# Loading later tiles of x one at a time, in halves from a second queue, with three regular output slots, in a pairwise bilinear kernel

## The chip, the cores and the metric

The kernel runs on one core of a Trainium2 chip. The metric is the device time of one execution in microseconds (us), taken without the profiler; the profile is of a separate execution and its span is measured from the first to the last instruction.

## What is computed

The input x has 4096 rows of 32 fields with 64 numbers each, W is 64 x 64, all float32. Every field is multiplied by W, and then every field i is multiplied, number by number, with the transformed field j for each of the 496 pairs i < j:

```python
vid = jnp.einsum('bfd,de->bfe', x, W)
idx_i, idx_j = jnp.triu_indices(F_, k=1)
return x[:, idx_i, :] * vid[:, idx_j, :]
```

The input is 33.6 MB and the output 520.1 MB, so writing the output is most of what the kernel moves.

## The kernel before

**Tiles.** The host lays x out so that the 128 partitions hold two batch halves of 64 embedding numbers, and so that a tile t (16 of them) holds 128 batch rows of each half. One field of one tile is a unit of 128 float32 per partition (512 B per partition, 64 KB in all). A tile of x is 32 units, its output 496 units (pairs).

**Memory.** One large SBUF tile, `mem` (L130), of 445 units holds both the tiles of x and the finished products waiting to be written. Where each tile of x lies is given by XPLACE (L25). Where each group of products (a slot) lies is given by the table SLOTS (L28), 80 pairs of (size in pairs, first unit): sizes run from 43 to 127 pairs, and places were fitted around the tiles of x that are in memory at the time. A slot's place is used again by later slots, and by tiles of x.

**Work on a tile** (loop at L155). TensorE multiplies the 32 fields by W, in 16 matmuls (two partition halves times eight banks, L162), into `vid`, one PSUM tile of 32 units, all of PSUM. VectorE multiplies (L186): `products` (L69) cuts the pairs of a tile into rectangular pieces, first all pairs among fields 0 to 15 (120 pairs), then fields 0 to 15 against 16 to 31 (256 pairs), then the pairs among fields 16 to 31 (120 pairs). A piece that would run over the end of a slot is cut there, so the slot table decides how many instructions there are (407). When the last pair of a slot is written, SyncE (SP) issues the slot's store (L189), one transfer with one row of up to 65,024 B per partition.

**Loads.** Every load also stands on SP's queue. The tiles of x come in the three groups of GROUPS (L20): the first group at the start (tile 0 in two halves with w between them, then tiles 1-2, 3-4 and 5, L138 to L153), the second (tiles 6-7 and 8-10) behind the products of tile 4, the third (tiles 12-11 and 15-13) behind those of tile 9 (L192 to L194). A load moves up to three tiles at once.

**Order.** SP's instructions keep the order in which the program writes them (`manual_schedule`, L122), so loads and stores form a single queue. Semaphore waits follow from overlaps: a product waits for the stores that still read its place, a load waits for the products and stores that use its place, a matmul waits for the products that still read its bank of `vid` and for its tile of x.

Of the kernel before, what the change touches and what calls it, by code (L numbers as in the profile page):

```python
# [16 lines left out]
UNITS = 445  # L17


GROUPS = [  # L20
    [[0], [1, 2], [3, 4], [5]],
    [[6, 7], [8, 9, 10]],
    [[12, 11], [15, 14, 13]],
]
XPLACE = [285, 317, 349, 381, 413, 0, 285, 317, 349, 381, 413, 128, 96, 64, 32, 0]  # L25


SLOTS = [  # L28
    (127, 32), (126, 159), (63, 32), (64, 95), (84, 159), (63, 32),
    (74, 243), (84, 159), (95, 32), (71, 243), (116, 127), (95, 32),  # L30
    (106, 243), (116, 127), (95, 32), (106, 243), (116, 127), (95, 32),
    (127, 243), (116, 127), (95, 32), (127, 243), (116, 127), (43, 370),
    (95, 32), (95, 127), (63, 222), (95, 32), (84, 127), (74, 211),
    (84, 32), (95, 116), (74, 211), (116, 0), (95, 116), (74, 211),
    (116, 0), (95, 116), (105, 211), (105, 0), (105, 105), (105, 211),
    (105, 0), (105, 105), (127, 211), (105, 0), (105, 105), (127, 211),
    (105, 0), (106, 105), (56, 211), (95, 267), (51, 362), (107, 160),
    (73, 267), (73, 340), (84, 160), (84, 244), (95, 340), (84, 160),
    (95, 244), (105, 340), (84, 160), (96, 244), (105, 340), (105, 128),
    (106, 233), (105, 339), (127, 96), (116, 223), (106, 339), (127, 96),  # L40
    (116, 223), (106, 339), (127, 64), (127, 191), (127, 318), (127, 32),
    (127, 159), (120, 286),
]


PAD = 24
# [2 lines left out]

STARTS = [0, *accumulate(n for n, _ in SLOTS)]  # L50


def by_block():


    def within(lo):
        yield "step", lo, 2, 1, 0
        for k in range(2):
            yield "step", lo, 4, 2, k
        for i in (lo, lo + 8):  # L60
            yield "row", i + 4, i, 4, 4
        yield "row", lo + 8, lo, 8, 8

    yield from within(0)
    yield "row", 16, 0, 16, 16
    yield from within(16)


def products(blocks, at=0):  # L69

    for kind, a, b, c, d in blocks:
        if kind == "row":
            rows, n, i0, di, j0, dj = c, d, b, 0, a, 1
        else:
            rows, n, i0, di, j0, dj = 16 // b, c, a, b, a + c + d, b
        r = k = 0
        while r < rows:
            room = STARTS[bisect_right(STARTS, at)] - at
            if k or room < n:
                m, w = 1, min(n - k, room)  # L80
            else:
                m, w = min(rows - r, room // n), n
            yield at, m, w, i0 + r * di + k, di, j0 + r * dj, dj
            at += m * w
            if k + w == n:
                r, k = r + m, 0
            else:
                k += w
# [10 lines left out]
@with_exitstack  # L99
def pairwise_bilinear_kernel(  # L100
    ctx: ExitStack,
    tc: tile.TileContext,
    x0: bass.AP,
    x: bass.AP,
    w: bass.AP,
    out: bass.AP,
):

    nc = tc.nc
    NT = sum(len(tiles) for group in GROUPS for tiles in group)
    F = x0.shape[1] - PAD0
    D = P // 2
    NP = F * (F - 1) // 2

    BANK = 512 // C


    ctx.enter_context(tc.manual_schedule(engines={mybir.EngineType.SP}))  # L122

    const = ctx.enter_context(tc.tile_pool(name="const", bufs=1))
    psum = ctx.enter_context(
        tc.tile_pool(name="ps", bufs=1, space=bass.MemoryType.PSUM)
    )
    vid = psum.tile([P, F, C], F32)

    mem = const.tile([P, UNITS, C], F32)  # L130


    w2 = const.tile([P, D], F32)


    for lo in (0, F // 2):
        place = XPLACE[0] + lo
        nc.sync.dma_start(out=mem[:, place : place + F // 2, :], in_=x0[:, lo : lo + F // 2, :])  # L138
        if lo == 0:
            nc.sync.dma_start(out=w2, in_=w)  # L140
    loaded = 1

    def load(tiles):
        nonlocal loaded
        n = len(tiles) * F
        place = XPLACE[tiles[0]]
        at = (loaded - 1) * F
        nc.sync.dma_start(out=mem[:, place : place + n, :], in_=x[:, at : at + n, :])
        loaded += len(tiles)

    groups = iter(GROUPS)
    for tiles in next(groups)[1:]:
        load(tiles)  # L153

    for t in range(NT):  # L155
        xt = mem[:, XPLACE[t] : XPLACE[t] + F, :]


        for b in range(0, F, BANK):
            for h in range(2):  # L160
                half = slice(h * D, (h + 1) * D)
                nc.tensor.matmul(  # L162
                    vid[half, b : b + BANK, :],
                    lhsT=w2[half, :],
                    rhs=xt[half, b : b + BANK, :],
                    start=True,
                    stop=True,
                )

        for at, m, w, i, di, j, dj in products(by_block(), t * NP):  # L170
            slot = bisect_right(STARTS, at) - 1
            n = m * w
            begin, end = STARTS[slot], STARTS[slot + 1]
            ot = mem[:, SLOTS[slot][1] : SLOTS[slot][1] + SLOTS[slot][0], :]
            o = ot[:, at - begin : at - begin + n, :]
            if m == 1:
                left = xt[:, i : i + w, :]
                right = vid[:, j : j + 1, :].to_broadcast([P, w, C])
            else:
                o = o.rearrange("p (m w) c -> p m w c", m=m)  # L180
                right = vid[:, j : j + (m - 1) * dj + 1 : dj, :].unsqueeze(2).to_broadcast([P, m, w, C])
                if di == 0:
                    left = xt[:, i : i + w, :].unsqueeze(1).to_broadcast([P, m, w, C])
                else:
                    left = xt.rearrange("p (m d) c -> p m d c", d=di)[:, i // di : i // di + m, i % di : i % di + w, :]
            nc.vector.tensor_tensor(o, left, right, ALU.mult)  # L186
            at += n
            if at == end:
                nc.sync.dma_start(out=out[:, begin:end, :], in_=ot)  # L189


        if t + 2 == loaded < NT:  # L192
            for tiles in next(groups):
                load(tiles)  # L194


_INS = ["r_x", "L0_rec_W"]
# [42 lines left out]
```

## Time and profile before

| | |
|---|---|
| time, median of 3 runs | 1288.43 us (1288.34 to 1288.59) |
| span of the profiled execution | 1287.0 us |
| VectorE busy | 1087.8 us (85%), 407 instructions |
| TensorE busy | 225.4 us (18%), 512 matmuls |
| DMA queue of SP | 553.69 MB, 12,960 packets, 99.7% of 16 engines' span |
| read from and written to HBM | 33.59 MB and 520.09 MB |

The page gives busy time of each compute engine, the busy share in 40 equal slices of the span, the bytes and time of each DMA queue, the chain of waits that ended last, and the costliest groups of instructions with what ended the idle time before them. A second view, of stages, gives for a stretch of the span the busy time of each engine, the clock granted to TensorE, the mean busy share of the 16 DMA engines and the GB/s they moved. The trace also holds a record of each single DMA packet: its queue, start, duration and bytes; a packet here is one partition's row of a transfer. Each transfer over 128 partitions is 8 packets on each of the 16 DMA engines and ends with one 4 B packet on each.

### The profile page before, as it was taken

How to read it: one execution, taken by the hardware profiler on the slowest of the kernel's cores; microseconds unless marked ns; L12 is line 12 of the kernel's file. 1: busy time of each engine (PE TensorE's matmuls, PEld its weight loads, DVE VectorE, ACT ScalarE, POOL GpSimd, SP SyncE). 2: the span in 40 equal slices, each digit the busy share in tenths (PEclk: the TensorE clock that was granted, in tenths of full speed). 3: DMA queues.
4: the chain of work that ended last, by engine and by line, in shares of the span. 5: the costliest groups of instructions: out<-in, count | busy, mean ns of one | idle time of the engine just before them, and what ended most of it. 6: DMA issues, size and time to landing. Idle time of an engine off the chain costs nothing.

```text
span 1287.0 us, 1744 instructions
## 1 busy us (share of the span) xinstructions
PE 225.4 (18%) x512; PEld 41.6 (3%) x512; DVE 1087.8 (85%) x407; POOL 0.2 (0%) x4
## 2 busy tenths in 40 slices
PE   4031221312013013030313111103131121302000
PEld 1000000000000000000000000000000000000000
DVE  6799999998948399899999887369999998989960
POOL 0000000000000000000000000000000000000000
PEclk8555555556555555565655555555555555655555
DMA  9999999999999999999999999999999999999998
GB/s 411 432 427 431 442 432 430 437 434 433 435 422 419 425 430 433 438 432 438 428 439 436 428 440 421 427 430 435 434 438 428 439 435 439 434 430 437 430 434 368
DMA packets 12969, 553.79 MB, mean 430 GB/s; under 512 B 1568, under 2 KB 1568, under 8 KB 1568
## 3 DMA queue, kind: packets, MB, share of 16 engines
q1 hardware_dynamic: 12960, 553.69, 99.7%
q8 instruction: 4, 0.07, 0.0%
q14 instruction: 5, 0.04, 0.0%
HBM read 33.59 MB, written 520.09 MB: 430 GB/s over the span
## 4 chain that ended last, share of the span: by engine, by line
DMA 49%; DVE 44%; issue 3%; PE 0%; another core or an unknown queue 0%; DVEq 0%; SPq 0%
DMA out_dram<-mem 49%; DVE mem L186 44%; PE vid L162 0%; DMA w<-in_L_rec_W_dram 0%; DVEq L228 0%; DVEq L186 0%; SPq L138 0%
## 5 line engine op out<-in xcount | busy, mean ns | idle before, releaser
L186 DVE TENSOR_TENSOR mem<-mem,vid 128x1024 f32<-128x1024 f32 (+16 forms) x407 | 1087.8, 2748 | 155.0 <-DMA out_dram<-mem 143.3
L162 PE MATMUL vid<-mem,w 64*64 64x512 f32 x512 | 225.4, 1004 | 949.5 <-DVE mem L186 883.2
L162 PEld LDWEIGHTS vid<-mem,w 64*64 64x64 f32 x512 | 41.6, 198 | 1131.6 <-DVE mem L186 1033.3
L208 POOL MEMSET const-bfloat16-1.0<- 128x1 bf16 x1 | 0.1, 101 | 0.0
L208 POOL MEMSET const-uint8-127<- 128x1 uint8 x1 | 0.1, 101 | 0.0
L208 POOL MEMSET const-float32-0.0<- 128x1 f32 x1 | 0.1, 98 | 0.2 <-issue 0.2
L208 POOL MEMSET const-float32-1.0<- 128x1 f32 x1 | 0.1, 98 | 0.0
## 6 DMA issues: line engine op xcount, KB each, us to landing
out_dram<-mem SPq DMA_DIRECT2D x12, 8128.0 KB, 35.1
out_dram<-mem SPq DMA_DIRECT2D x13, 6720.0 KB, 32.9
out_dram<-mem SPq DMA_DIRECT2D x14, 6080.0 KB, 31.0
out_dram<-mem SPq DMA_DIRECT2D x9, 7424.0 KB, 31.6
out_dram<-mem SPq DMA_DIRECT2D x8, 5376.0 KB, 23.7
out_dram<-mem SPq DMA_DIRECT2D x6, 6784.0 KB, 34.6
out_dram<-mem SPq DMA_DIRECT2D x4, 4736.0 KB, 26.2
mem<-in_r_x_dram SPq DMA_DIRECT2D x4, 4096.0 KB, 21.8
```

The lines of the kernel that those rows point to most:

```text
L162: nc.tensor.matmul(vid[half, b : b + BANK, :], lhsT=w2[half, :], rhs=xt[half, b : b + BANK, :], start=True, stop=True,)
L186: nc.vector.tensor_tensor(o, left, right, ALU.mult)
L208: nc = _bacc.Bacc("TRN2", target_bir_lowering=False, num_devices=1, dynamic_dma_scratch_size=1024)
```

## The change

Only the first five tiles are loaded at the start, all on SP as before. Each of the other eleven is loaded on its own, in two halves of 16 fields (1 MB, rows of 8 KB per partition), and these 22 loads are issued from ScalarE's queue, which otherwise has nothing to do. A half is issued as soon as the half that lay in its place has been used for the last time: fields 0 to 15 after 376 pairs of a tile (the first two blocks), fields 16 to 31 at the end of it. From tile 5 on there are two places for x, used in turn, so tile t+2 goes where tile t was; tiles 5 and 6 take the places of tiles 0 and 1.

The slots become regular: three of equal size, used in turn. While the first tiles still hold memory they have 95, then 105 and 116 pairs, from tile 5 on 127, which with two places for x fill the 445 units. The host no longer permutes the tiles. What is computed, and the order of pairs in a tile, stay the same.

```diff
-GROUPS = [
-    [[0], [1, 2], [3, 4], [5]],
-    [[6, 7], [8, 9, 10]],
-    [[12, 11], [15, 14, 13]],
-]
-XPLACE = [285, 317, 349, 381, 413, 0, 285, 317, 349, 381, 413, 128, 96, 64, 32, 0]
-SLOTS = [
-    (127, 32), (126, 159), (63, 32), (64, 95), (84, 159), (63, 32),
...
-]
+HEAD = [[0], [1], [2, 3, 4]]
+FIRST_HALF = 376
+
+def place_of(t):
+    return (381, 413, 285, 317, 349)[t] if t < 5 else (381, 413)[(t - 5) % 2]
+
+def slots():
+    n = 0
+    left = 16 * 496
+    out = []
+    while left:
+        done = n // 496
+        room = (95, 95, 95, 105, 116)[done] if done < 5 else 127
+        k = len(out) % 3
+        size = min(room, left)
+        out.append((size, k * room))
+        n += size
+        left -= size
+    return out
+
+SLOTS = slots()
...
-    ctx.enter_context(tc.manual_schedule(engines={mybir.EngineType.SP}))
+    ctx.enter_context(tc.manual_schedule(engines={mybir.EngineType.SP, mybir.EngineType.Activation}))
...
-    def load(tiles):
-        nonlocal loaded
-        n = len(tiles) * F
-        place = XPLACE[tiles[0]]
-        at = (loaded - 1) * F
-        nc.sync.dma_start(out=mem[:, place : place + n, :], in_=x[:, at : at + n, :])
-        loaded += len(tiles)
-
-    groups = iter(GROUPS)
-    for tiles in next(groups)[1:]:
-        load(tiles)
+    def load(queue, tile, lo, n):
+        place = place_of(tile) + lo
+        at = (tile - 1) * F + lo
+        queue.dma_start(out=mem[:, place : place + n, :], in_=x[:, at : at + n, :])
+
+    for tiles in HEAD[1:]:
+        load(nc.sync, tiles[0], 0, len(tiles) * F)
+
+    later = {}
+    for t in range(5, NT):
+        before = t - 5 if t < 7 else t - 2
+        later.setdefault(before, t)
...
             nc.vector.tensor_tensor(o, left, right, ALU.mult)
             at += n
+            if at == t * NP + FIRST_HALF and t in later:
+                load(nc.scalar, later[t], 0, F // 2)
             if at == end:
                 nc.sync.dma_start(out=out[:, begin:end, :], in_=ot)
...
-        if t + 2 == loaded < NT:
-            for tiles in next(groups):
-                load(tiles)
+        if t in later:
+            load(nc.scalar, later[t], F // 2, F // 2)
...
-    x = x[:, [t for group in GROUPS for tiles in group for t in tiles]]
```

## The prediction

> **What bounds the kernel now.** I read the page first, slices before shares. Its second part shows the 16 DMA engines full in all slices, VectorE (DVE) with holes:
>
> ```profile
> DVE  6799999998948399899999887369999998989960
> ...
> DMA  9999999999999999999999999999999999999998
> GB/s 411 432 427 431 442 432 430 437 434 433 435 422 419 425 430 433 438 432 438 428 439 436 428 440 421 427 430 435 434 438 428 439 435 439 434 430 437 430 434 368
> DMA packets 12969, 553.79 MB, mean 430 GB/s; under 512 B 1568, under 2 KB 1568, under 8 KB 1568
> ```
>
> The rate is flat near 433 GB/s but for four places: the first slice, the 12th to 14th, the 25th and 26th, and the last (a slice is 32 us). The third and fourth parts say whose bytes these are and that the end hangs on them:
>
> ```profile
> q1 hardware_dynamic: 12960, 553.69, 99.7%
> ...
> HBM read 33.59 MB, written 520.09 MB: 430 GB/s over the span
> ...
> DMA 49%; DVE 44%; issue 3%; PE 0%; another core or an unknown queue 0%; DVEq 0%; SPq 0%
> ```
>
> The chain's 44% of DVE is no second bound: it hops over DVE because a store cannot be issued before its products exist, while older stores keep the engines busy. Of DVE's idle time before L186 (155.0 us) 143.3 us wait for a store to free a slot. So each microsecond of DMA time added or removed arrives at the end one for one, and only that.
>
> The trace's single packets give the price. A 65,024 B store packet takes 2,400 ns, one of 32,256 B 1,194 ns: 0.03677 ns per byte plus 8 ns per packet; the 4 B packet that signals a transfer's end takes 9 ns. Per engine: 553.69 MB / 16 x 0.03677 = 1272.4 us, 90 transfers x 8 packets x 8 ns = 5.8 us, 90 x 9 ns = 0.8 us: 1279.0 us. The first packet starts at 2.6 us, the last ends 0.6 us before the span's end. The packets' excess over this price, summed and divided by 16, is 4.7 us. Together 1286.9 us, against a span of 1287.0 (1288.4 as timed).
>
> **Where the excess sits** answers what a read among writes costs. It is 0.9 us in the opening loads; nearly all the rest lies in the two later visits to the loads: 1.97 us from 380 to 440 us, 1.18 us from 800 to 840 us. In each, the last store packets before the loads and the last load packets before the stores take about 0.9 us too long on every engine (at the second visit's entry less). The stages show it too (columns: stage, its length, busy times, PE clock, DMA share, GB/s):
>
> ```profile
> 30.00:380.00 350.00, 65.60 (x142) 10.52 (x138) 314.67 (x125) 0.00 (x0) 0.53 1.00 433
> 380.00:426.00 46.00, 10.09 (x24) 2.65 (x24) 33.01 (x15) 0.00 (x0) 0.54 1.02 421
> 426.00:800.00 374.00, 64.90 (x144) 11.10 (x144) 332.52 (x125) 0.00 (x0) 0.53 1.00 433
> 800.00:833.00 33.00, 6.13 (x16) 1.77 (x16) 13.09 (x3) 0.00 (x0) 0.55 1.02 424
> ```
>
> 421 for 433 GB/s over 46 us is 1.3 us lost, 424 over 33 us 0.7 us. "Busy" stays at 1.00: a turn from writing to reading counts as busy time, so only GB/s and packet durations reveal it.
>
> The trace also holds nine reads that another queue slipped between stores:
>
> ```profile
> q8 instruction: 4, 0.07, 0.0%
> q14 instruction: 5, 0.04, 0.0%
> ```
>
> (five of 8 KB, four of 16 KB, once the program runs). At 143.4 us an 8 KB fetch keeps one engine for 0.31 us, its transfer alone, but the engine's next store takes 2,151 instead of 1,796 ns, 0.36 us more. Three of the other 8 KB fetches cost 0.35 or 0.36 us in the same way, one 0.27. A 16 KB fetch lasts 0.88 to 0.96 us instead of 0.61, and the next store loses 0.38 to 0.41 us more: some 0.7 us. At 164.1 us the fetch stands between two packets of one and the same store (59,392 B on both sides, and only one such transfer near): a second queue gets in after a packet, not after a transfer.
>
> **What the Trainium skill says.** "DMA: Bandwidth & Descriptors", section "Where 436 GB/s comes from", puts the ceiling of the fabric at 435.2 GB/s; the trace agrees (433 to 434 in stages of stores alone; 0.03677 ns per byte is 435). Its section "Issuing engines are not separate DMA queues" says that transfers from several issuing engines share the same 16 DMA engines and interleave: ScalarE's queue brings no bandwidth. Its section "Queues, rings and completion order" says that an engine goes round-robin over queues with work, at packet granularity, and that a packet is typically 9 to 17 descriptors. The fetch at 164.1 us shows a switch inside a transfer, so I take single records of the trace as the unit; whether the 8 records of an 8 KB-row load stay together, no trace here shows.
>
> **The change part by part.**
>
> 1. Slots: 80 stores become 68; SLOTS gives 16 of 95 pairs, 5 of 105, 4 of 116, 42 of 127, one of 93. Same bytes. Loads go from 9 and one for w to 26 and one: 95 transfers instead of 90, so 5 x (8 x 8 + 9) ns = 0.4 us more.
> 2. DVE: 379 products instead of 407 (counted from both slot tables). From the 128- and 1,024-element rows (283 and 1,214 ns) the fixed part is 0.15 us: 28 x 0.15 = 4 us less. Hidden: DVE has 155 us of idle time.
> 3. Starving the DMA: DVE fills 127 pairs in 17.4 us (first stretch, 11.5 to 29.0 us); their store takes 8 x 2.40 = 19.2 us. While DVE refills one of three slots, two stores (38.4 us) are queued, so 17.4 us plus some 2 us of launch (0.7 us issue to 2.6 us first packet) fits. Where slots grow, a new one overlaps the second old one only with its last 11 to 22 pairs, some 3 us of DVE beside at least 14 us of queued store. Cost 0.
> 4. Start: 5 tiles queued instead of 6. Before, 12.6 MB of loads end near 33.9 us; 2.1 MB less ends near 29. The first slot of 95 pairs is full at 11.5 + 95 x 0.138 = 24.6 us and its store can begin near 26.5. Cost 0, with 2 us to spare. Tile 5's bytes only move.
> 5. The added wait: a load on ScalarE waits for the last DVE product (and matmul) that reads its half tile. Behind it on ScalarE stand only later loads; stores stay on SP. The half is needed one tile later, at least 70 us, and lands after 8 x (2.40 + 0.31 + 0.36) = 25 us even if it alternates with stores. No one waits. Cost 0.
> 6. The two visits go: 3.2 us less.
> 7. The price: 22 loads of 1 MB, each 8 packets of 8 KB per engine, in a second queue while the store queue is never empty. If each packet gets in singly, 22 x 8 = 176 reads per engine are inserted among stores. At 0.36 us each: 63 us; at the 0.7 us of the 16 KB fetches: 123 us; if reads already queued are prefetched behind a 2.4 us store, perhaps 0. I take 0.36: same packet size, and a second queue as here.
>
> Sum: 1288.4 + 0.4 - 3.2 + 63 = 1348.6; I say 1348.
>
> **The rivals.**
> - Loads stay together: each engine drains the 8 packets of a load before it goes back. Then 22 visits at the 1.58 us mean of the two measured: 35 us, 1288.4 + 35 - 3 = 1320. With 0.36 us a visit 1293, with 1.97 us 1329. For it: the skill's packet of several descriptors. Against: the fetch inside a store.
> - Costly singles: 0.7 us each, 1288 + 123 - 3 = 1408. For it: all 16 engines now turn at once, as in the visits. Against: no 8 KB fetch cost more than 0.36.
> - Hidden turns: with two queues one engine reads ahead while it writes; no cost per load, and the visits' 3.2 us are saved: 1288.4 + 0.4 - 3.2 = 1285.6, just faster than before; with the opening's excess gone too 1284.7. No more can be won, for 1279 us is bytes. For it: the fetch's own record shows no latency. Against: the store after it does. If half the saving is lost, the time stays within 0.2%.
>
> **How the numbers follow.** Singles at 0.36 to 0.5 us (1345 to 1375): 0.45. Costly singles (to 1413): 0.13. Loads together (1293 to 1329): 0.29. Little or no cost, within 0.2%: 0.07. Faster: 0.05. Anything above 1413: 0.01. The range, 1306 to 1413, leaves out the last three and the cheap end of "together", some 0.07. Slower 0.88, same 0.07, faster 0.05.
>
> **What would show it.** DVE's busy time near 1084 us, its waits still for stores, no wait of PE for loads: steps 2 to 5. The DMA share still 9 in every slice, but GB/s near 405 in the tiles that load (0, 1 and 5 to 13) and 433 in tiles 2 to 4, 14 and 15, mean near 411: step 7. Packets: 8 KB loads near 0.31 us, the store after each 0.36 us too long, load and store alternating on an engine. Eight loads in a row mean the first rival; 433 GB/s throughout means hidden turns. Slices with DMA below 9 mean starving, and step 3 or 4 is wrong.

## The result and the profile after

The changed kernel takes 1295.7 us (1295.4 to 1297.2), the kernel before, run beside it, 1288.5 us. The ratio is 1.0057, with a 95% interval of 1.0043 to 1.0071: slower by 7.2 us, where 60 us were forecast.

From the page of the changed kernel, the lines that answer to those shown of before (the last line is from the view of its DMA issues):

```profile
DVE  6998889599799999788787888888888878789860
...
DMA  9999999999999999999999999999999999999997
GB/s 406 435 427 438 427 431 433 433 421 429 437 437 430 440 405 457 406 457 419 424 450 423 432 415 451 422 431 436 431 426 428 421 437 441 422 450 418 450 418 327
DMA packets 13689, 553.79 MB, mean 428 GB/s; under 512 B 1648, under 2 KB 1648, under 8 KB 1648
...
q1 hardware_dynamic: 10512, 530.62, 95.2%
q10 hardware_dynamic: 3168, 23.07, 4.2%
...
HBM read 33.59 MB, written 520.09 MB: 428 GB/s over the span
...
DMA 56%; DVE 33%; issue 8%; PE 0%; DVEq 0%; SPq 0%
...
L187 DVE TENSOR_TENSOR mem<-mem,vid 128x1024 f32<-128x1024 f32 (+15 forms) x379 | 1087.4, 2940 | 165.7 <-DMA out_dram<-mem 154.0
...
mem<-in_r_x_dram ACTq DMA_DIRECT2D x22, 1024.0 KB, 27.0
```

The queues are full until the end and VectorE still waits for stores (154.0 us, before 143.3). The bytes are the same; q10 is ScalarE's queue. The mean rate fell only from 430 to 428 GB/s: the tiles that load do not run at 405 as step 7 said. The view by stages (stage, length, busy times, PE clock, DMA share, GB/s) has a stretch without loads first, then tiles 5 to 13, which load:

```profile
270.00:440.00 170.00, 26.80 (x64) 5.09 (x64) 161.72 (x56) 0.00 (x0) 0.55 1.00 434
443.00:1146.00 703.00, 132.24 (x288) 24.59 (x288) 598.12 (x206) 0.00 (x0) 0.55 1.00 431
```

What stands out is the last slice, 327 GB/s against 368. The same view shows that end. First the kernel before, then the changed one:

```profile
1240.00:1283.00 43.00, 0.00 (x0) 0.00 (x0) 2.83 (x1) 0.00 (x0) 0.50 0.98 426
1283.00:1287.00 4.00, 0.00 (x0) 0.00 (x0) 0.00 (x0) 0.00 (x0) 0.50 0.04 15
```

```profile
1265.00:1283.00 18.00, 0.00 (x0) 0.00 (x0) 0.00 (x0) 0.00 (x0) 0.50 0.93 401
1283.00:1286.00 3.00, 0.00 (x0) 0.00 (x0) 0.00 (x0) 0.00 (x0) 0.50 0.51 222
1286.00:1290.00 4.00, 0.00 (x0) 0.00 (x0) 0.00 (x0) 0.00 (x0) 0.50 0.33 143
1290.00:1293.60 3.60, 0.00 (x0) 0.00 (x0) 0.00 (x0) 0.00 (x0) 0.50 0.03 13
```

(A packet's time is booked where the packet starts, so the share falls up to 2.4 us before an engine is done. The times of single packets, here and in the prediction, stand 0.8 us above those of the views: the first packet, 2.6 us in the prediction, starts after 1.7 us in the views.) Before, the 16 DMA engines finish within 3.6 us of each other. After, the share is already down to half at 1283 us, and others work on for up to 10 us. Each engine's closing 4 B packets date this: in the last store before, the engines end at 1284.0 us on average and the last at 1286.5 us; after, at 1287.1 us on average and the last at 1293.2 us. Of the 6.8 us of later end, 3.1 us are the average engine's and 3.7 us are more unevenness than before: eight engines end within 0.4 us of each other, the others 3 to 10 us later. Every store is cut evenly over 16 engines, so the slowest engine sets the end.

The closing packets of earlier stores show when the engines drift apart. The last engine is 1.3 us behind the first at 438 us, when the loads of tiles 5 to 13 begin, and 3.2 us at 646 us, 5.2 us at 810 us, 7.7 us at 974 us, 9.5 us at 1138 us. After the last load it stays at 9.5 us. (The four loads in tiles 0 and 1 had raised it to 4.2 us; a pause of the engines at 267 us, of which more under step 3, took most of that back.) Without the later loads it is never above 2.4 us. So it is the loads, and lag adds up on the slower engines.

### The profile page after: what moved, and what is told of

Read it like the earlier page. It is cut to its first block, busy times and chain, and to the rows that moved or that the text cites. A ratio compares the mean times of both kernels' runs of the same rounds, so it can differ in the third digit from the quotient of the medians.

```text
span 1293.6 us, 1776 instructions
## 1 busy us (share of the span) xinstructions
PE 225.1 (17%) x512; PEld 42.6 (3%) x512; DVE 1087.4 (84%) x379; POOL 0.2 (0%) x4
## 4 chain that ended last, share of the span: by engine, by line
DMA 56%; DVE 33%; issue 8%; PE 0%; DVEq 0%; SPq 0%
DMA out_dram<-mem 55%; DVE mem L187 33%; PE vid L163 0%; DMA w<-in_L_rec_W_dram 0%; DVEq L229 0%; DVEq L187 0%; SPq L140 0%
## 5 line engine op out<-in xcount | busy, mean ns | idle before, releaser
L187 DVE TENSOR_TENSOR mem<-mem,vid 128x1024 f32<-128x1024 f32 (+15 forms) x379 | 1087.4, 2940 | 165.7 <-DMA out_dram<-mem 154.0
```

## The experiments

All times are medians, with a run of the kernel before on the same chip at 1288.6 to 1288.7 us.

**Without the later loads.** Both calls for tiles 5 to 15 are left out, so these tiles are computed from what lies in their places and the output is not right; stores and products are the same:

```diff
             if at == t * NP + FIRST_HALF and t in later:
-                load(nc.scalar, later[t], 0, F // 2)
+                pass
...
-            load(nc.scalar, later[t], F // 2, F // 2)
+            pass
```

> The changed kernel without its 22 later loads: tiles 5 to 15 use what lies in the two places (tiles 0 and 1), so their output is not the reference's. All stores, slots and products stay. The bytes left out take 23.07 MB / 16 x 0.03677 ns = 53.0 us, the packets' fixed parts 1.6 us. Theory A (the loads' turns cost some 9 us on the slowest engine): 1295.7 - 54.6 - 9 = 1232 us (1231 to 1234). Rival B (slots are the reason, and the loads cost their bytes alone): 1241 us.

Measured: 1233.0 us, ratio 0.9569 (0.9554 to 0.9583). The loads cost 62.7 us, of which bytes and packets explain 54.6 us: 8.1 us are left. The engines stay together (mean end 1229.5 us, last 1230.5 us). Adding 54.6 us gives 1284.1 and 1285.1 us, against 1287.1 and 1293.2 us with the loads. So the loads cost the average engine 3.0 us and the slowest 8.1 us beyond their bytes; the timed difference is the slowest engine's. Over 176 reads that is 0.046 us each on the slowest, and on average 0.017 us at most: some 0.8 of the 3.0 us are the pause at 267 us, which is shorter here (step 3). The time without loads gives a floor for what follows: 1233.0 + 53.0 us of bytes + 0.073 us per load: 1287.6 us with 22 loads, 1286.8 with 11, 1289.2 with 44.

**Slots of 95 pairs throughout.**

```diff
-        room = (95, 95, 95, 105, 116)[done] if done < 5 else 127
+        room = 95
```

> The changed kernel with slots of 95 pairs throughout (84 stores of 48,640 B rows instead of 68 of up to 65,024 B): no slot grows, so no new slot overlaps two old ones. 16 more stores of 8 packets add 16 x (64 + 9) ns = 1.2 us. Theory A with the first four loads' price (1.0 us on the slowest engine for four loads among stores of 95 pairs, where 18 loads among stores of 127 pairs cost 8.5 us): 18 x 0.25 = 4.5 instead of 8.5 us, 1293 us. If a load costs the same beside shorter stores: 1297 us. Rival B (growth of slots starves the engines, some 1 to 1.5 us of the mean engine): that goes, 1295 us. If three slots of 95 are too few, DVE's waits for stores stay but the DMA share falls below 9 in some slices and the time rises above 1300 us.

Measured: 1295.7 us, ratio 1.0056 (1.0040 to 1.0073), which is 1293.8 to 1298.0 us, the same as the changed kernel. The 1293 us that shorter stores were to give did not come. Rival B's 1295 us and the 1297 us of unchanged loads both lie inside, so the time alone does not clear the growth of the slots. The packets do in the main: this kernel has no pause at 267 us, where the engines of the changed kernel stand idle for 0.9 us on average, and that is about what its 1.2 us of more stores take back. Growth is thus worth about 1 us, not the 7.2 us.

**The same 22 half loads in SP's queue.**

```diff
-                load(nc.scalar, later[t], 0, F // 2)
+                load(nc.sync, later[t], 0, F // 2)
...
-            load(nc.scalar, later[t], F // 2, F // 2)
+            load(nc.sync, later[t], F // 2, F // 2)
```

> The changed kernel with its 22 later half loads issued from SP's queue instead of ScalarE's; everything else stays. Theory A (a second queue hides most of a turn between writing and reading, because an engine can fetch the queued read behind a store packet; in one queue each visit to a load costs what the visits before the change cost, 1.2 to 2.0 us): the second queue's share of the cost, some 9 us on the slowest engine, goes and 22 x 1.58 = 35 us comes, 1321 us, at the least 22 x 1.18 - 9 = 17 us more, 1313 us. Rival C (each load costs the same whichever queue it is in, only the number of loads counts): 1296 us, within 2 us. Rival B (the extra time comes from the slots, not from the loads): 1296 us as well.

Measured: 1302.8 us, ratio 1.0107 (1.0092 to 1.0122): 7.1 us slower than in ScalarE's queue, so the queue matters, though less than theory A said. Over the floor it is 15.2 us, 0.69 us for each of 22 visits. Its last 20 us:

```profile
1280.00:1286.00 6.00, 0.00 (x0) 0.00 (x0) 0.00 (x0) 0.00 (x0) 0.50 0.72 313
1286.00:1291.00 5.00, 0.00 (x0) 0.00 (x0) 0.00 (x0) 0.00 (x0) 0.50 0.31 133
1291.00:1301.80 10.80, 0.00 (x0) 0.00 (x0) 0.00 (x0) 0.00 (x0) 0.50 0.11 48
```

For the last 10.8 us the DMA share is 0.11, which is two of 16 engines. The average engine ends at 1289.3 us, 12 us before the last. Unevenness is thus the form that a turn's cost takes in one queue as well.

**Whole loads in SP's queue, at the end of a tile** (11 visits with 16 KB rows):

```diff
-                load(nc.scalar, later[t], 0, F // 2)
+                pass
...
-            load(nc.scalar, later[t], F // 2, F // 2)
+            load(nc.sync, later[t], 0, F)
```

> The changed kernel with each later tile loaded in one piece at the end of the tile whose place it takes, on SP's queue: 11 visits with 16 KB rows in one queue. In one queue, 22 visits with 8 KB rows gave 1302.8 us. If a visit has its price (the slowest engine lost 0.74 us in each of the 22): 11 fewer visits, 1302.8 - 8.1 = 1294.7 us. If the row's size sets the price of a visit, as it seems to in a second queue: 0.74 x 2 = 1.5 us a visit, 1303 us.

Measured: 1295.0 us, ratio 1.0052 (1.0037 to 1.0067), 8.2 us over the floor: 0.75 us a visit. Half the visits cost about half; had the price gone by bytes, this run would have come to some 1302 us. A price per read packet would fit too, for these are halved as well (88 for 176); the next two runs part the two.

**Two tiles to a visit, three places for x, slots of 116** (6 visits, SP's queue):

```diff
-    return (381, 413, 285, 317, 349)[t] if t < 5 else (381, 413)[(t - 5) % 2]
+    return (381, 413, 285, 317, 349)[t] if t < 5 else (381, 413, 349)[(t - 5) % 3]
...
-        room = (95, 95, 95, 105, 116)[done] if done < 5 else 127
+        room = (95, 95, 95, 105, 116)[done] if done < 5 else 116
...
-        before = t - 5 if t < 7 else t - 2
-        later.setdefault(before, t)
+        before = 1 if t < 7 else t - 2 - (t + 1) % 2
+        later.setdefault(before, []).append(t)
...
-            if at == t * NP + FIRST_HALF and t in later:
-                load(nc.scalar, later[t], 0, F // 2)
...
-        if t in later:
-            load(nc.scalar, later[t], F // 2, F // 2)
+        for tile in later.get(t, []):
+            load(nc.sync, tile, 0, F)
```

> The changed kernel with three places for x instead of two, slots of 116 instead of 127 pairs from tile 5 on, and the later tiles loaded two at a time, whole, on SP's queue: 6 visits instead of 11 (with 11 visits on SP's queue: 1295.0 us) or 22 (1302.8 us). Without later loads the kernel takes 1233.0 us, their bytes and packets 53.8 us: 1286.8 us before turns; the 11 visits then cost 0.75 us each, the 22 (with 0.8 us more of packets) 0.69 us each. Theory V (a visit of one queue to the loads has a price, whatever it loads): 1286.8 + 4 stores more (0.3) + 6 x 0.72 = 1291.4 us. Rival W (each load has its price): 1295.3 us.

Measured: 1293.0 us, ratio 1.0034 (1.0021 to 1.0047), which is 1291.4 to 1294.7 us beside this run's 1288.7. Theory V's 1291.4 us lies on the edge, rival W's 1295.3 us outside. Over its floor of 1287.1 us it is 5.9 us, 0.7 to 1.3 us a visit with the interval: fewer visits help, with the same 11 loads and 88 read packets per engine; whether a visit with two loads costs more than one with a single load, this doesn't tell.

**The kernel before with its two later groups in rows of 8 KB** (20 loads at the same two moments):

```diff
-        nc.sync.dma_start(out=mem[:, place : place + n, :], in_=x[:, at : at + n, :])
+        step = n if loaded < 6 else F // 2
+        for k in range(0, n, step):
+            nc.sync.dma_start(out=mem[:, place + k : place + k + step, :], in_=x[:, at + k : at + k + step, :])
```

> The kernel before with its two later groups of loads cut into half loads of 16 fields (8 KB rows, 1 MB each, 20 loads instead of 4), still on SP's queue and at the same two moments. 16 more loads add 16 x (8 x 8 + 9) ns = 1.2 us. If the row's size sets what a turn costs, most of the two visits' 3.2 us goes: 1286.5 to 1287.5 us. If all engines turning in step sets it, whatever the rows, the visits keep their 3.2 us: 1289.8 us.

Measured: 1288.4 us, ratio 0.9999 (0.9990 to 1.0007). It lies between the two: 1.2 us of packets more and 0.2 us less time, so about 1.4 us of turns saved, with an interval of over 1 us to each side. With 160 read packets per engine instead of 32 the same two visits cost no more, so in one queue the price does not go by the packet. The size of the rows does not explain most of what a visit costs, and no version came of it that is faster beyond doubt.

**The kernel before with its later groups in ScalarE's queue** (whose order is then the program's, as in the changed kernel).

```diff
-    ctx.enter_context(tc.manual_schedule(engines={mybir.EngineType.SP}))
+    ctx.enter_context(tc.manual_schedule(engines={mybir.EngineType.SP, mybir.EngineType.Activation}))
...
-        nc.sync.dma_start(out=mem[:, place : place + n, :], in_=x[:, at : at + n, :])
+        queue = nc.sync if loaded < 6 else nc.scalar
+        queue.dma_start(out=mem[:, place : place + n, :], in_=x[:, at : at + n, :])
```

> The kernel before, with its two later groups of loads (4 transfers of 4 or 6 MB) issued from ScalarE's queue, at the same places in the program; slots, places and opening loads stay. Theory A (a second queue hides the turn): the two visits' 3.2 us of excess mostly go, 1285.5 to 1287 us. Rival E (alternation itself costs; each of the 32 read packets per engine is now inserted singly): between 0.05 and 0.36 us each, 1288 to 1297 us.

Measured: 1289.9 us, ratio 1.0008 (0.9999 to 1.0016), no gain. With reads of 32 and 48 KB a second queue hides nothing that the time shows.

**Other sizes and moments in ScalarE's queue.** Whole loads (11, rows of 16 KB), at the end of the tile:

```diff
-                load(nc.scalar, later[t], 0, F // 2)
+                pass
...
-            load(nc.scalar, later[t], F // 2, F // 2)
+            load(nc.scalar, later[t], 0, F)
```

> The changed kernel with each later tile loaded in one piece of 2 MB at the end of the tile whose place it takes, on ScalarE's queue: 11 loads instead of 22, 88 read packets of 16 KB per engine instead of 176 of 8 KB. Theory A with a price for each inserted read packet: the some 9 us that the loads cost on the slowest engine are halved, 1291 us (1290 to 1292). Rival B (slots): unchanged, 1295 to 1296.5 us. Rival D (price per byte read, or per tile): unchanged too.

Measured: 1299.2 us, ratio 1.0077 (1.0060 to 1.0094). Half as many reads cost more, 12.4 us over the floor instead of 8.1. None of the theories had that. Quarter loads (44, rows of 4 KB):

```diff
-            load(nc.scalar, later[t], F // 2, F // 2)
+            load(nc.scalar, later[t], F // 2, F // 4)
+            load(nc.scalar, later[t], 3 * F // 4, F // 4)
```

(and the same for the first half.)

> The changed kernel with each half load split into two of 8 fields (4 KB rows), issued one behind the other at the same moments on ScalarE's queue: 44 loads, 352 read packets per engine. Theory A with a price for each inserted read packet: twice the some 9 us, 1304 us (1301 to 1307), of which 176 x 8 ns + 22 x 9 ns = 1.6 us are the packets' own fixed part. Rival B or D (slots, or price per byte): 1297 us.

Measured: 1294.8 us, ratio 1.0046 (1.0031 to 1.0061), 5.6 us over a floor that is itself 1.6 us higher. Part of that is not the price of reads: at 1092 to 1101 us the engines stand idle for 2.3 us on average, because a store waits for a load with which it shares a completion semaphore (the run with lone reads below shows more of this):

```profile
SPq L193 <- DMA mem<-in_r_x_dram: 66.8, 2, 33.7
```

(columns: who waited for whom: us in total, times, longest.) So a price per inserted packet, the form that step 7 gave it, is refuted twice: 88 reads cost 12.4 us, 176 cost 8.1, 352 cost 5.6. To part size from moment, two half loads at the tile's end:

```diff
-                load(nc.scalar, later[t], 0, F // 2)
+                pass
...
+            load(nc.scalar, later[t], 0, F // 2)
             load(nc.scalar, later[t], F // 2, F // 2)
```

> The changed kernel with the first half load of each tile moved from pair 376 to the end of the tile, so that both halves (still two loads with 8 KB rows on ScalarE's queue) follow each other. It stands between the changed kernel (1295.7 us) and the one with whole loads at the end (1299.2 us, 16 KB rows). Theory F (the size of a read packet sets what its insertion costs: 4 KB the least, 16 KB the most): 1295 to 1296.5 us, as the changed kernel. Rival G (the moment of issue, later and all at once, is what made whole loads slower): 1299 us. If only the number of separate stretches of alternation counts, it is faster than the changed kernel, 1292 us.

Measured: 1297.1 us, ratio 1.0075 (1.0058 to 1.0092). It lies between; the intervals of all three overlap in part, so size and moment are not cleanly parted.

**Another pitch of x in HBM.**

```diff
-    x = _np.pad(x[:, 1:].reshape(2 * D, (NT - 1) * F, C), ((0, 0), (0, PAD), (0, 0)))
+    x = _np.pad(x[:, 1:].reshape(2 * D, (NT - 1) * F, C), ((0, 0), (0, 8), (0, 0)))
```

> The changed kernel with x laid out in HBM with rows of 488 instead of 504 units (pitch 249,856 B instead of 258,048 B); nothing on the chip changes but the addresses that the loads read. Theory A (what a turn costs comes from an engine changing between writing to and reading from HBM, wherever the read lies): 1295.7 us, within 1 us. Rival H (where the reads of 16 engines fall in HBM makes some engines wait, and the same ones each time): moves by 2 us or more, either way.

Measured: 1297.6 us, ratio 1.0072 (1.0057 to 1.0087): 1.9 us more, between the two bounds, with an interval that overlaps that of the changed kernel. Inconclusive.

**Reads one at a time.**

```diff
+    def load_piece(tile, lo, g):
+        place = place_of(tile) + lo
+        at = (tile - 1) * F + lo
+        rows = slice(16 * g, 16 * g + 16)
+        nc.scalar.dma_start(out=mem[rows, place : place + F // 2, :], in_=x[rows, at : at + F // 2, :])
+
+    pieces = []
...
-            if at == t * NP + FIRST_HALF and t in later:
-                load(nc.scalar, later[t], 0, F // 2)
+            if pieces:
+                load_piece(*pieces.pop(0))
...
-            load(nc.scalar, later[t], F // 2, F // 2)
+            pieces += [(later[t], half * F // 2, g) for half in range(2) for g in range(8)]
```

> The changed kernel with each half load cut into 8 transfers of 16 partitions (one 8 KB read packet per DMA engine each), still on ScalarE's queue; one of them is issued after each of the first 16 products of the tile that follows, so that most reads stand alone between stores, as the instruction fetches do, with no second read queued behind them. The same 176 reads per engine; 154 more transfers add 154 x 9 ns = 1.4 us. Theory L (a lone read costs what a fetch costs, 0.36 us; reads queued in a row hide it): up to 63 us, 1340 to 1350 us. Rival M (a read of x among stores is cheap whether or not others are queued behind it, and the fetch was no measure for it): 1295 to 1299 us.

Measured: 1315.1 us, ratio 1.0208 (1.0191 to 1.0225), between the two theories and within neither; the time alone would mislead. The waits of SP's queue show why:

```profile
SPq L199 <- DVE mem L194: 623.0, 45, 26.3
SPq L199 <- DMA mem<-in_r_x_dram: 414.2, 30, 42.4
```

In this kernel stores wait for loads. The trace shows eight completion semaphores that serve the transfers of both queues in turn; a transfer is issued only when the one that had its semaphore before has landed. With 16 small loads to a tile that is often a load (47 of the 66 such waits of stores, against 14 of 66 in the changed kernel, where no store was held up by a load). The store queue runs dry, and the reads go on by themselves:

```profile
446.00:458.00 12.00, 4.12 (x8) 0.76 (x8) 12.00 (x9) 0.00 (x0) 0.50 1.05 430
458.00:468.00 10.00, 5.38 (x10) 1.06 (x10) 10.00 (x6) 0.00 (x0) 0.50 0.92 188
```

At 0.92 busy the engines move 188 GB/s: reads of 8 KB that follow each other with no store between take 0.6 to 0.8 us. Of the 176 reads per engine 47 take over 0.5 us, 0.69 us on average, 18.2 us above their price in all; that is nearly all of the 19.4 us by which this kernel is slower than the changed one. The reads that did stand alone, with over 3 us to the next on both sides as far as packets can be put to engines, take 0.31 us, and the store after one loses some 0.04 us on average. So a lone read of x is as cheap as one in a row: rival M, once the starvation is set aside.

## Why the prediction was wrong

**The bound and the direction held, the direction partly by luck.** DMA bytes set the time, a turn costs time that the busy share does not show, and the changed kernel is slower. But it is slower by another way than the one forecast, which had 63 us on every engine and no unevenness.

**Steps 1, 2, 4 and 5 held in the main.** There are 379 products and the 95 transfers counted. The first store is issued at 24.85 us (24.6 forecast), the DMA share is 9 in every slice but the last. A load lands 27.0 us after issue (25 forecast from strict alternation). TensorE does wait for x, less than before (60.1 us then), but VectorE waits for TensorE only once, at the start:

```profile
PE vid L163 <- DMA mem<-in_r_x_dram: 35.9, 8, 6.4
DVE mem L187 <- PE vid L163: 11.6, 1, 11.6
```

One side term was off: DVE saved 0.4 us instead of 4 (1087.4 for 1087.8 us), which no one waits for. Summed one by one the products did become 4.0 us shorter (1114.4 for 1118.4 us), but neighbours overlap by some 80 ns, and fewer products overlap less (27.1 us in all for 30.6 us); busy time counts an overlap once.

**Step 3 overlooked one wait.** It said that a grown slot waits for the second old one only with its last 11 to 22 pairs, and put the cost at 0. But a product waits as a whole. Where slots grow from 95 to 105 pairs, a product of 64 pairs reaches 3 units into the second old slot, and waits 10.9 us for its store:

```profile
L187 DVE TENSOR_TENSOR mem<-mem,vid 128x8192 f32<-128x8192 f32 x17 | 147.6, 8681 | 10.9 <-DMA out_dram<-mem 10.9
```

The next store is issued at 267.1 us, too late: by the packets, the engines stand idle there for 0.9 us on average (and 0.1 us at 365 us), which slices of 32 us do not show. The kernel before has no such pause, the one without later loads 0.2 us in all. Its cost is a share of the average engine's 3.1 us; what the slowest engine lost by it is not known.

**Step 7 failed: the price of an inserted read, 0.36 us, taken from the instruction fetches.** The first half of the step was right: single packets alternate. A load of 8 packets per engine takes 15 to 20 us in the changed kernel, seven stores and eight reads long, where 2.5 us would do in a row; the packet of several descriptors, named for the rival of loads that stay together, is not what the engines drained here. But a read of x takes 0.309 us, just its bytes, and in most of the cases where the store behind it can be told apart that store loses less than 0.01 us; on average it loses some 0.04 us. The fetches in the same execution keep their price: the store behind a fetch at 140.2 us takes 2,151 ns instead of 1,796, as before. So the 0.36 us belongs to instruction fetches, not to any read among stores. The runs show that these differ, not why. I had the two ends in hand (0.36 us, and 0 for reads that go on behind a store) and chose the wrong one, on the ground of equal packet size.

**The rival "hidden turns" was nearer, and missed unevenness.** It put the time at 1285.6 us. Without the loads, plus bytes and packets, comes 1287.6 us (of the 2.0 us between the two only 0.2 us, the pause, is accounted for); the average engine then loses 3.0 us. But every step here reckoned with an average over 16 engines. The slowest loses 8.1 us, and it sets the end. Even before, the last engine ended 2.5 us after the average one; that the balance still came to 1286.9 for 1287.0 us was luck, for the packets' durations, 1284.0 us per engine, overlap by 2.7 us.

**The rival "loads stay together" failed in its size too.** The one-queue runs show what a visit costs: 0.69 to 1.0 us (the pause of step 3 counted in), not the 1.58 us read from before's two visits. Those 1.58 us were the packets' excess averaged over the engines, with all engines in both visits reading 4 or 6 MB transfers one behind another. Why the average there is higher than the end-to-end price of visits with small loads stays open.

**Where the 7.2 us came from**, then: the changed kernel trades two visits in one queue for 22 short ones in a second. At the price of one queue, 22 visits would have cost 14 us more (1302.8 us); the second queue gives back half of that. It does not bring 22 visits down to the cost of two. No version tried is faster than the kernel before, and with its bytes at 1272 us there is little left to win.

**Open:** why some engines lose and others nothing at all, why larger reads cost more in the second queue, and whether it is always the same engines (the records carry no engine number; that the last engine's lag grows from load to load speaks for it). The run with another pitch does not rule out that it matters where in HBM the reads fall. The 8.1 us follow the loads and, in one queue, the number of visits; that each visit's turn from writing to reading is what delays the slow engines is argued from this, not seen in single packets.

## What to carry to other kernels

When DMA bytes set the time, count how often the stream turns from writing to reading, and load in few large visits if memory allows; where many small loads can't be avoided, a second queue can lower the cost of their turns: here it halved it with packets of 8 KB (8.1 for 15.2 us), and with packets of 16 KB it seems to have raised it (12.4 for 8.2 us, with intervals that just overlap). Reckon with the slowest of the 16 engines, not with the mean: look at the DMA share in the last stages, where a tail at a few tenths is lag that has added up over the whole kernel. Where slots overlap older ones, reckon with the whole instruction that touches the overlap, not with its last pairs. And take a price only from an event of the same kind: a fetch of instructions among stores is no measure for a load.

## What was not expected of the hardware

Reads of 8 KB inserted between 65 KB stores from a second queue cost at most 0.017 us each on the average engine beyond their bytes, while a fetch of 8 KB costs 0.36 us in the same kernel. The engines of one core end 9.6 us apart (16 us with the loads in SP's queue) though every transfer is cut evenly. Reads of one 8 KB packet per engine, with nothing else in the queues, take 0.6 to 0.8 us each instead of 0.31.
